# Attention rounds of five score units, the order of the expert tiles, and the end stage of a fused transformer block

## Chip, cores and metric

The kernel runs on one core of one Trainium2 chip. The metric is the device time of one execution in microseconds, lower is better. All times below are of that kind, or come from one profiled execution of the kernel.

## The reference

The inputs are `query` (1, 2048, 512) and the weights; everything is float32. Cut to what matters:

```python
xn = layernorm(x)
x = x + attention(xn, Wq, Wk, Wv, Wout, lambdas, rms_weight) + ffn(xn, gate, w1, w3, w2, sw1, sw3, sw2)

def attention(xn, ...):                       # H = 16 heads, two maps each, D = 16
    q, k = rotary(xn @ Wq), rotary(xn @ Wk)   # (T, 2H, D)
    v1, v2 = (xn @ Wv).reshape(T, H, 2, D)
    attn1 = softmax(causal(q1 k1 / sqrt(D))) @ [v1, v2]
    attn2 = softmax(causal(q2 k2 / sqrt(D))) @ [v1, v2]
    f = rfft(attn1, over T) - lambda_full * rfft(attn2, over T)
    a = irfft(f * gaussian(frequency))
    a = a * rsqrt(mean(a * a, per head) + eps) * rms_weight * (1 - lambda_init)
    return a.reshape(T, 512) @ Wout

def ffn(x, ...):                              # 8 experts, best 2 of each token, width 352
    y = sum of topk_w * w2[e] (silu(w1[e] x) * w3[e] x)
    return y + (silu(x @ sw1) * (x @ sw3)) @ sw2     # shared expert, width 704
```

## The kernel before, in words

There are three stages. The first (0 to about 210 us) does the layer norm, the gate, the routing of tokens to experts and the projections to q, k and v. The third, `ending`, does the filter over time as a folded transform, the norm per head, the output projection and the sums with the experts' results. The stage between, `middle`, mixes attention with the experts and is where most of the change lies. In it the order of the instructions on TensorE (PE), VectorE (DVE), ScalarE (ACT), GpSimd (POOL) and the queue of SyncE (SP) is as the program issues them; in `ending` the same holds for all but SP.

**Attention units.** The 32 chunks (8 groups of two heads by 4 blocks of 512 queries) give a stream of 544 *units*. A unit is mostly one head, one block of 128 keys and 512 queries, for both maps of the differential attention. `Chunk.scores` (L822) makes it with two matmuls of 64 rows, side by side in the array, into a tile `ps_s` of two PSUM banks (pool `sc_ps`, two tiles, so four banks). One exp on ACT (L835) writes `pt`, of which the pool `prob` has eight; units on the diagonal of the mask then have `affine_select` on POOL (L840). `Chunk.values` (L862) multiplies `pt` with v into `ps_o`, four matmuls of 32 columns for one key block. `Chunk.added` (L876, L879) sums the probabilities on DVE. At the end of a chunk, `sums` (L888, L893) and `finish` (L900 to L908: two transposes, a reciprocal, and `o_n`) normalize it, and `put` (L917, POOL) writes it over `vd`. After that `folded` (POOL) does, in small steps of a generator, the first butterflies of the transform for a finished group of heads.

**Experts.** The generator `experts` first does tiles of the shared expert (`wh` L246, tanh and products L256/L257/L263, `wy` L284) and then the 34 tiles of the routed experts: tiles 0 to 27 hold 128 tokens of one expert, tiles 28 to 33 hold 64 tokens each of two experts. A tile goes through `xT` (transposed rows, L165), `xh` and `xg` (L180), `ps_u` and `uT` (L206 to L209), `xy` (L216), `y_sb` (L225) and a store to `ys` (L228). There are two places for weights, `w_sb`; `fetch_up` (L146, `wu`, 1408 KB) and `fetch_down` (L149, `wd`, 768 KB) fill one from `wex` as soon as its last reader is done, on SP's queue, two fetches ahead. A tile of two experts uses both places. The generator yields a weight of work after each piece.

**Banks.** All the experts' results in PSUM (`xh`, `xg`, `ps_u`, `xy`, `ps_x`, and the attention's `ps_sum`, `ps_ot`, `ps_st`) rotate through three banks (pool `f_ps`, function `bank`). One bank is for `ps_o`.

**Rounds.** The loop at the end of `middle` takes the stream in rounds of four units: two units of scores (`burst(units[:2])`), the values of earlier units, the sums of a chunk that ends, two more units, the remaining values, then `put` and `finish`, then the adds on DVE, mixed with one or more steps of expert work, as many as keep the share of work done at the share of the stream done. The adds of unmasked units stand ahead of and between these steps, the masked ones behind them. Last come up to two steps of `folded`. Once attention has ended, the rest of the experts' steps follow without it.

**The end stage.** `ending` opens pools of its own over the memory of `middle`. It makes a last tile of the shared expert (`kept` holds its inputs), the products with the filter (`ps_z`, L1141) with butterflies on DVE around them, and then a loop of eight steps over pairs of output tiles: `prepared` (next pair: L1163, L1219, L1243 to L1254), `means` (L1223 to L1227), `scales` (L1234), `across` (transposes, L1262/L1264), `projected` (L1270) and `finished` (L1275, add and store). The residual and the experts' results arrive in tiles `res`, of which there are twelve: `fetched` loads the query rows on SP (L1120), adds `ysh` (L1123) and gathers twice from `ys` (L1125) with DMAs on POOL. `still` issues those of the last four tiles inside the loop.

Of the kernel before, what the change touches and what calls it, by code (L numbers as in the profile page):

```python
# [8 lines left out]
F32 = mybir.dt.float32  # L9
# [37 lines left out]

NP = (T * TOP // HALF - NX) // 2
WUP = NE * 2 * FI
WCOL = WUP + NF * E  # L50
# [17 lines left out]
def block_kernel(  # L68
# [527 lines left out]
    def middle(general):  # L596


        with ExitStack() as pools:
# [29 lines left out]
            def experts():  # L629
# [7 lines left out]
                for t0 in range(EARLY, NT - 1, TQ):  # L637
                    t1 = min(t0 + TQ, NT - 1)
                    last = t1 == NT - 1
                    cols = slice(t0 * P, t1 * P)  # L640
                    for n, us in enumerate(chunks(xnT[:, :, cols], u_last)):
                        if last and n == 0:
                            who_sb = mp.tile([P, E], F32, tag="x", name="who_sb")
                            who_sb = who_sb[:NR].rearrange("n (k p o) -> n k p o", k=TOP, o=2)
                            for k in range(TOP):
                                nc.sync.dma_start(who_sb[:, k], who[k][: NR * P, :].rearrange("(n p) o -> n p o", p=P))
                        elif last and n == 2:
                            nc.vector.tensor_add(who_sb[:, 0], who_sb[:, 0], who_sb[:, 1])
                        elif last and n == 3:
                            ps = bank([P, 2, NR], "ps_w")  # L650
                            for i in range(2):
                                nc.tensor.transpose(ps[:, i, :], who_sb[:, 0, :, i], ident[:NR, :NR])
                            nc.vector.tensor_copy(tok, ps[:, 0, :])
                            nc.vector.tensor_copy(wcol, ps[:, 1, :])
                        elif last and n == 5:


                            xr = [rows_of(0), rows_of(1)]
                            es = [routed(0)]
                            fetch_up(es[0], 0, nc.sync)  # L660
                        yield 3.45 * (t1 - t0) / TQ
                    if last:
                        es.append(routed(2))
# [20 lines left out]
                def tile_down(j, uT):  # L684
                    return places(j, 1), uT, ys[j * P : (j + 1) * P, :], wcol[:, j : j + 1]

                for j in range(NR):
# [5 lines left out]
                    if j + 2 < NR:  # L693
                        xr.append(rows_of(j + 2))
                    for n in sets[j]:
# [61 lines left out]
            def greatest(g, qc):  # L757
# [29 lines left out]
                return shift  # L787

            class Chunk:

# [19 lines left out]

                def scores(self, unit):

                    g, qc = self.g, self.qc
                    if general and not self.probs:
                        self.shift = greatest(g, qc)
                    ps = sps.tile([P, 2, QC], F32, tag="sc", name="ps_s")
                    for h, kb, off, col, w in unit:
                        for s in range(2):
                            r = slice(64 * s, 64 * s + 64)
                            k = keys[2 * g + h, kb // TQ][r, kb % TQ * P : (kb % TQ + 1) * P]  # L820
                            to = ps[:, s, col : col + w]
                            nc.tensor.matmul(  # L822
# [11 lines left out]
                    used = slice(min(c for *_, c, _ in unit), max(c + w for *_, c, w in unit))  # L834
                    nc.scalar.activation(pt[:, :, used], ps[:, :, used], AF.Exp, scale=SCALE)  # L835
                    for _, kb, _, col, _ in unit:
                        if kb >= qc * TQ and not general:

                            part = pt[:, :, col : col + P]
                            nc.gpsimd.affine_select(  # L840
                                out=part, in_=part, pattern=[[0, 2], [1, P]], compare_op=ALU.is_ge, fill=0.0,
                                base=0, channel_multiplier=-1,
                            )
# [147 lines left out]
            def burst(units):  # L991
                nonlocal begun
                found = []
                for n, chunk, unit in units:
# [21 lines left out]

            def masked(entry):
                _, c, unit = entry
                return any(kb >= c.qc * TQ for _, kb, *_ in unit)

            def added(entries):
# [6 lines left out]

            for i in range(0, len(stream), 4):
                units = stream[i : i + 4]  # L1030
                found = burst(units[:2])
# [19 lines left out]
                added(before)  # L1051
                added(u for u in units[:2] if not masked(u))
                later = [u for u in units[2:] if not masked(u)]
                while True:
                    work()
                    added(later[:1])
                    later = later[1:]
                    if worked / (work_all - left) >= (i + 4) / len(stream):
# [32 lines left out]
    def ending():  # L1091

        with tc.tile_pool(name="tail1", bufs=1) as t1, tc.tile_pool(name="tail", bufs=2) as tp, tc.tile_pool(
            name="tail_ps", bufs=4, space=PSUM
        ) as fps, tc.tile_pool(name="conv_ps", bufs=2, space=PSUM) as zps, tc.manual_schedule(
            engines={mybir.EngineType.PE, mybir.EngineType.DVE, mybir.EngineType.Activation, mybir.EngineType.Pool}
# [53 lines left out]
            def copied(z):  # L1152
                diff = tp.tile([P, 2, E], F32, tag="diff", name="diff")
                nc.scalar.copy(diff, z)
# [27 lines left out]
            product(zr[:, 1, :], [(1, vd[:, 1, :])])  # L1182
            first = tp.tile([P, E], F32, tag="first", name="first", bufs=1)
            nc.scalar.copy(first, zr[:, 1, :])
# [127 lines left out]
            for n in range(NT // 2):  # L1312
# [157 lines left out]
```

## Time and profile before

| what | value |
|---|---|
| time before, median of 3 | 1358.39 us (1357.41 to 1359.54) |
| profiled execution, its own time | 1360.14 us |
| its span | 1358.3 us |
| PE busy, share of the span | 1312.6 us, 97% |
| DVE, ACT, POOL busy | 74%, 51%, 46% |
| granted TensorE clock | 0.994 |
| HBM read and written | 169.69 MB and 43.10 MB |
| first stage, attention with experts, end stage | 0 to 210, 210 to 1241, 1241 to 1358 us |

The profile is of one execution. Busy time of an engine counts its instructions, not the issue of DMAs. PEld is the load of a matmul's weights, which runs beside PE. In the kernel's names, `ps_s<-qS,kS` means that `ps_s` is made from `qS` and `kS`; L822 is line 822 of the kernel before. A row that names a releaser tells whose end came last before the waiting instruction began.

### The profile page before, as it was taken

The numbers are of one execution on the slowest core, as the hardware profiler recorded it, in microseconds if no ns is written. First come the engines' busy times: TensorE is split into PE (matmuls) and PEld (weight loads), VectorE is DVE, ScalarE is ACT, GpSimd is POOL, SyncE is SP. The second block draws the span as 40 slices with busy tenths as digits, with TensorE's granted clock in tenths as the row PEclk, the third lists the DMA queues.
The fourth block names the chain that finished last, engine by engine and source line by source line (L and its number), as shares of the span: only waits on it lengthen the run. The fifth ranks groups of instructions, "written<-read, shape, count | busy, mean of one in ns | idle before, by whom it ended". The sixth has DMA issues, their size and how long they took to land.

```text
span 1358.3 us, 20810 instructions
## 1 busy us (share of the span) xinstructions
PE 1312.6 (97%) x7554; PEld 600.3 (44%) x7554; DVE 1005.4 (74%) x1344; ACT 688.4 (51%) x847; POOL 626.3 (46%) x671
## 2 busy tenths in 40 slices
PE   7999999999999999999999999899999999987998
PEld 3444444334443444445444444344544444443544
DVE  7049883287668778868889986778898788764785
ACT  2311110265656566676666666566676666640221
POOL 0002330012221323235968984778589469421764
PEclk9999999999999999999999999999999999998999
DMA  9406673200211122235665656555565666777997
GB/s 375 171 16 171 201 196 97 89 15 32 75 43 31 40 75 82 74 123 170 190 194 143 226 176 180 181 173 174 185 194 178 210 189 230 262 294 293 175 219 169
DMA packets 75578, 214.29 MB, mean 158 GB/s; under 512 B 12244, under 2 KB 12696, under 8 KB 69576
## 3 DMA queue, kind: packets, MB, share of 16 engines
q1 hardware_dynamic: 62744, 185.68, 41.7%
q0 software_dynamic: 11056, 22.78, 8.6%
q10 hardware_dynamic: 1664, 4.38, 0.9%
q8 instruction: 63, 1.03, 0.3%
q14 instruction: 51, 0.42, 0.1%
HBM read 169.69 MB, written 43.10 MB: 157 GB/s over the span
## 4 chain that ended last, share of the span: by engine, by line
PE 65%; DVE 6%; POOL 5%; DMA 3%; issue 1%; ACT 1%; SPq 0%; DVEq 0%; ACTq 0%; POOLq 0%
PE ps_o L862 16%; PE ps_s L822 12%; PE wh L246 8%; PE xy L216 6%; PE xg L180 5%; PE xh L180 5%; PE wy L284 4%; PE ps_sum L888 2%; DMA wu<-in_wex_dram 2%; POOL pt L840 1%; PE po L1270 1%; DMA wd<-in_wex_dram 1%; DVE sum L879 1%; PE ps_ot L900 1%; PE ps_x L165 1%
## 5 line engine op out<-in xcount | busy, mean ns | idle before, releaser
L879 DVE TENSOR_TENSOR sum<-sum,pt 128x1024 f32<-128x1024 f32 (+3 forms) x576 | 621.4, 1128 | 36.3 <-ACT pt L835 21.6
L835 ACT ACTIVATE pt<-ps_s 128x1024 f32<-128x1024 f32 x544 | 527.3, 1023 | 184.3 <-PE ps_s L822 131.0
L840 POOL TENSOR_SCALAR_AFFINE_SELECT pt<-pt 128x256 f32<-128x256 f32 x256 | 171.0, 693 | 358.7 <-ACT pt L835 357.5
L862 PE MATMUL ps_o<-pt,vd 128*32 128x512 f32 (+3 forms) x2560 | 268.0, 534 | 4.1 <-POOL pt L840 4.1
L822 PE MATMUL ps_s<-qS,kS 64*128 64x512 f32 (+3 forms) x1280 | 203.8, 406 | 2.0 <-DVEq L1335 1.6
L822 PEld LDWEIGHTS ps_s<-qS,kS 64*128 64x128 f32 x1280 | 97.1, 185 | 177.0 <-issue 95.9
L246 PE MATMUL wh<-xnT,wu 128*128 128x512 f32 (+1 forms) x352 | 150.4, 574 | 0.0
L862 PEld LDWEIGHTS ps_o<-pt,vd 128*32 128x32 f32 x2560 | 66.9, 109 | 125.8 <-issue 103.5
L545 PE MATMUL ps_x<-xnT,wqk_sb 128*128 128x512 f32 x256 | 110.5, 593 | 0.0
L498 POOL DMA_INDIRECT who<-pairs,slot x32 | 33.1, 1034 | 165.9 <-DVE pairs L495 104.9
L216 PE MATMUL xy<-wd,uT 128*128 128x512 f32 (+3 forms) x240 | 97.1, 606 | 7.7 <-DVE rcp L903 6.3
L246 PEld LDWEIGHTS wh<-xnT,wu 128*128 128x128 f32 x352 | 64.1, 190 | 72.7 <-issue 56.5
L180 PE MATMUL xh<-wu,xT 128*128 128x352 f32 (+1 forms) x320 | 90.5, 473 | 4.2 <-DMA wu<-in_wex_dram 3.3
L917 POOL TENSOR_TENSOR vd<-o_n 128x128 f32<-128x128 f32 x60 | 62.2, 1057 | 65.6 <-DVE o_n L908 65.5
L180 PE MATMUL xg<-wu,xT 128*128 128x352 f32 (+1 forms) x320 | 88.6, 468 | 0.0
L545 PEld LDWEIGHTS ps_x<-xnT,wqk_sb 128*128 128x128 f32 x256 | 48.4, 190 | 60.6 <-issue 60.6
L284 PE MATMUL wy<-wd,ws 128*128 128x512 f32 x160 | 74.8, 603 | 0.0
L257 DVE SCALAR_TENSOR_TENSOR ws<-ws,wh 128x512 f32<-128x512 f32 (+4 forms) x26 | 16.7, 644 | 73.6 <-ACT ws L256 73.6
L1125 POOL DMA_INDIRECT res<-ys,slot x32 | 54.9, 1715 | 25.3 <-DMA res<-ysh 13.5
L562 ACT CAST hi<-turned 128x1024 fp32r<-128x1024 f32 x16 | 16.7, 1045 | 93.9 <-DVE turned L560 70.9
L180 PEld LDWEIGHTS xh<-wu,xT 128*128 128x128 f32 (+1 forms) x320 | 48.0, 176 | 31.7 <-issue 6.5
L180 PEld LDWEIGHTS xg<-wu,xT 128*128 128x128 f32 (+1 forms) x320 | 46.6, 174 | 34.4 <-issue 14.8
(254 smaller groups left out, 1416.8 us busy)
## 6 DMA issues: line engine op xcount, KB each, us to landing
wu<-in_wex_dram SPq DMA_DIRECT2D x44, 1408.0 KB
wd<-in_wex_dram SPq DMA_DIRECT2D x43, 768.0 KB
kS<-parts_k SPq DMA_DIRECT2D x128, 128.0 KB
qS<-parts_q SPq DMA_DIRECT2D x256, 64.0 KB
ys<-y_sb SPq DMA_DIRECT2D x34, 256.0 KB
parts_q<-hi SPq DMA_DIRECT2D x32, 256.0 KB
parts_k<-hi SPq DMA_DIRECT2D x16, 256.0 KB
parts_k<-turned SPq DMA_DIRECT2D x16, 256.0 KB
```

The lines of the kernel that those rows point to most:

```text
L180: nc.tensor.matmul(dst[r, :], xT[:, c, r], w[:, o : o + FI], start=(c == 0), stop=(c == NE - 1), skip_group_check=True,)
L216: nc.tensor.matmul(y[r, :], uT[:m, ic, r], w[:m, ic * E : (ic + 1) * E], start=(ic == 0), stop=(ic == NF - 1), skip_group_check=True,)
L246: nc.tensor.matmul(dst, w_sb[o // WUP][0][:, o % WUP : o % WUP + P], x[:, c, :], start=(c == 0), stop=(c == NE - 1))
L284: nc.tensor.matmul(y, us[i][:, t * P : (t + 1) * P], w_sb[i // NF][1][:, i % NF * E : (i % NF + 1) * E], start=(i == 0), stop=(i == SCH - 1),)
L545: nc.tensor.matmul(ps[:, i, :], wqk_sb[st, qk][:, i, c, :], xnT[:, c, cols], start=(c == 0), stop=(c == NE - 1),)
L822: nc.tensor.matmul(to, k, queries[2 * g + h, qc][r, off : off + w], start=True, stop=not general)
L835: nc.scalar.activation(pt[:, :, used], ps[:, :, used], AF.Exp, scale=SCALE)
L840: nc.gpsimd.affine_select(out=part, in_=part, pattern=[[0, 2], [1, P]], compare_op=ALU.is_ge, fill=0.0, base=0, channel_multiplier=-1,)
L862: nc.tensor.matmul(self.o[r : r + 32, off:], vd[:, kb, v0 : v0 + 32], pt[:, s, :], start=first, stop=self.ended, skip_group_check=True,)
L879: nc.vector.tensor_add(to, to, pt)
L917: eng.tensor_add(vd[:, self.qc * TQ : (self.qc + 1) * TQ, v0 : v0 + 32], self.o_n[:, :, h, 0, :], self.o_n[:, :, h, 1, :],)
L1125: nc.gpsimd.indirect_dma_start(out=came[k], out_offset=None, in_=ys, in_offset=bass.IndirectOffsetOnAxis(ap=slot[:, step - 2, order[k] : o ...
```

## The change

**Rounds.** A round takes five units where no chunk is being closed (`closing` is empty), else four. The second burst then has three units, and the first of these is made "apart": its two score matmuls go to two banks of `f_ps` (`ps_a`) in place of a tile of `sc_ps`, and its exp is two instructions of one bank each. 84 rounds have five units; there are 115 rounds where there were 136.

**Adds and fold steps.** The adds of a round's first two units all stand ahead of the expert work, masked ones too. The steps of `folded` are one for an unmasked round and one more if the next four units are unmasked. A unit with two parts at columns 0 and 256 has one `affine_select` in place of two.

**Order of tiles.** `ORDER` puts the six tiles of two experts ahead of the last two tiles of one expert. One fetch of `wd` more is issued.

**End stage.** The tiles `ws`, `diff` and `first` come from a pool of their own, `tail2`, which is opened ahead of `tail`; `y_sb` is written by ACT; three operations of `prepared(4)` move to `prepared(3)`; in the loop, `finished` and `still` of an odd tile go ahead of `across` and `prepared`, and `means` goes behind `finished` of the even one. Nine of the sixteen `wh` products of the first group stand behind the last `xy` in PE's order; before, all sixteen stood ahead of it.

```diff
+ORDER = [*range(NP - 2), *range(NP, NR), *range(NP - 2, NP)]
...
-                sets = [[j] if j < NP else [2 * j - NP, 2 * j - NP + 1] for j in range(NR)]
-                halves = [2 * j + i for j in range(NR) for i in range(len(sets[j]))]
+                sets, halves = [], []
+                for tj in ORDER:
+                    n = 1 if tj < NP else 2
+                    sets.append(range(len(halves), len(halves) + n))
+                    halves += [2 * tj + i for i in range(n)]
...
-                    ps = sps.tile([P, 2, QC], F32, tag="sc", name="ps_s")
+                    if apart:
+                        banks = [bank([P, QC], "ps_a") for _ in range(2)]
+                    else:
+                        ps = sps.tile([P, 2, QC], F32, tag="sc", name="ps_s")
+                        banks = [ps[:, s] for s in range(2)]
...
-                    nc.scalar.activation(pt[:, :, used], ps[:, :, used], AF.Exp, scale=SCALE)
+                    if apart:
+                        for s in range(2):
+                            nc.scalar.activation(pt[:, s, used], banks[s][:, used], AF.Exp, scale=SCALE)
+                    else:
+                        nc.scalar.activation(pt[:, :, used], ps[:, :, used], AF.Exp, scale=SCALE)
...
-                    found += chunk.scores(unit)
+                    found += chunk.scores(unit, k == len(units) - 3)
...
-            for i in range(0, len(stream), 4):
-                units = stream[i : i + 4]
+            upto = 0
+            while upto < len(stream):
+                many = 4 if general or closing else 5
+                units = stream[upto : upto + many]
+                upto += many
...
-                added(u for u in units[:2] if not masked(u))
-                later = [u for u in units[2:] if not masked(u)]
+                added(units[:2])
+                later = [u for u in units[2:] if not masked(*u[1:])]
...
-                added(u for u in units if masked(u))
-                if any(map(masked, units)) or not shared:
-                    steps = 0
-                else:
-                    steps = 1 if any(map(masked, stream[i + 4 : i + 8])) else 2
-                for _ in range(steps):
+                added(u for u in units[2:] if masked(*u[1:]))
+                steps = [
+                    shared and not any(masked(*u[1:]) for u in some) for some in (units, stream[upto : upto + 4])
+                ]
+                for _ in range(sum(map(bool, steps))):
...
-            _, _, _, _, (_, _, stored), _ = expert(tp, fps)
-            hidden, gated, times, _, result = shared_expert(tp, fps, 2)
+            _, _, _, _, (_, _, stored), _ = expert(tp, fps, by_scalar=True)
+            hidden, gated, times, _, result = shared_expert(t2, fps, 2)
...
-                elif n == 4:
+                elif n == 3:
                     nc.vector.tensor_sub(dv, zw, dv)
                     scaled(v1[:, 0], dv[:, 1], TAN8, dv[:, 0])
                     scaled(v1[:, 1], dv[:, 0], -TAN8, dv[:, 1])
+                elif n == 4:
...
+                if ahead is not None:
+                    finished(2 * n - 1, ahead)
+                    still(2 * n - 1)
                 if n + 1 < NT // 2:
                     aT = across(2 * n + 2)
                 if n + 2 < NT // 2:
                     pairs.append(prepared(n + 2))
-                if ahead is not None:
-                    finished(2 * n - 1, ahead)
-                    still(2 * n - 1)
-                if n + 2 < NT // 2:
-                    pairs[n + 2].means()
                 if n + 1 < NT // 2:
                     now, po = po, projected(after)
                     finished(2 * n, now)
                     still(2 * n)
+                if n + 2 < NT // 2:
+                    pairs[n + 2].means()
```

More of the change, by code (lines that the diff above doesn't have):

```diff
@@ L655, in experts @@
                         elif last and n == 5:
-                            xr = [rows_of(0), rows_of(1)]
-                            es = [routed(0)]
+                            xr = [rows_of(j) for j in ORDER[:2]]
+                            es = [routed(2 * ORDER[0])]
                             fetch_up(es[0], 0, nc.sync)
@@ L662, in experts @@
                     if last:
-                        es.append(routed(2))
+                        es.append(routed(2 * ORDER[1]))
                         fetch_up(es[1], 1, nc.sync)
@@ L684, in tile_down @@
                 def tile_down(j, uT):
-                    return places(j, 1), uT, ys[j * P : (j + 1) * P, :], wcol[:, j : j + 1]
+                    tj = ORDER[j]
+                    return places(j, 1), uT, ys[tj * P : (tj + 1) * P, :], wcol[:, tj : tj + 1]
                 for j in range(NR):
@@ L693, in experts @@
                     if j + 2 < NR:
-                        xr.append(rows_of(j + 2))
+                        xr.append(rows_of(ORDER[j + 2]))
                     for n in sets[j]:
@@ L787, in greatest, with masked @@
                 return shift
+            def masked(chunk, unit):
+                return any(kb >= chunk.qc * TQ for _, kb, *_ in unit)
             class Chunk:
@@ L809, in units, with scores @@
                             yield [(h, kb, 0, 0, QC)]
-                def scores(self, unit):
+                def scores(self, unit, apart):
                     g, qc = self.g, self.qc
@@ L820, in scores @@
                             k = keys[2 * g + h, kb // TQ][r, kb % TQ * P : (kb % TQ + 1) * P]
-                            to = ps[:, s, col : col + w]
+                            to = banks[s][:, col : col + w]
                             nc.tensor.matmul(
@@ L834, in scores @@
                     used = slice(min(c for *_, c, _ in unit), max(c + w for *_, c, w in unit))
-                    nc.scalar.activation(pt[:, :, used], ps[:, :, used], AF.Exp, scale=SCALE)
-                    for _, kb, _, col, _ in unit:
-                        if kb >= qc * TQ and not general:
-                            part = pt[:, :, col : col + P]
+                    if apart:
[3 more added lines that the diff above has]
+                        nc.scalar.activation(pt[:, :, used], ps[:, :, used], AF.Exp, scale=SCALE)
+                    if masked(self, unit) and not general:
+                        cols = [col for *_, col, _ in unit]
+                        if cols == [0, 2 * P]:
+                            chosen = [pt.rearrange("p s (h q) -> p (s h) q", h=2)[:, :, :P]]
+                        else:
+                            chosen = [pt[:, :, col : col + P] for col in cols]
+                        for part in chosen:
                             nc.gpsimd.affine_select(
-                                out=part, in_=part, pattern=[[0, 2], [1, P]], compare_op=ALU.is_ge, fill=0.0,
-                                base=0, channel_multiplier=-1,
+                                out=part, in_=part, pattern=[[0, part.shape[1]], [1, P]], compare_op=ALU.is_ge,
+                                fill=0.0, base=0, channel_multiplier=-1,
                             )
@@ L993, in burst @@
                 found = []
-                for n, chunk, unit in units:
+                for k, (n, chunk, unit) in enumerate(units):
                     if n > begun:
@@ L1015, in work @@
                 worked += next(ex, work_all)
-            def masked(entry):
-                _, c, unit = entry
-                return any(kb >= c.qc * TQ for _, kb, *_ in unit)
             def added(entries):
@@ L1057, in middle @@
                     later = later[1:]
-                    if worked / (work_all - left) >= (i + 4) / len(stream):
+                    if worked / (work_all - left) >= upto / len(stream):
                         break
                 added(later)
-                added(u for u in units if masked(u))
-                if any(map(masked, units)) or not shared:
-                    steps = 0
-                else:
-                    steps = 1 if any(map(masked, stream[i + 4 : i + 8])) else 2
-                for _ in range(steps):
+                added(u for u in units[2:] if masked(*u[1:]))
[3 more added lines that the diff above has]
+                for _ in range(sum(map(bool, steps))):
                     if folding is None and ready:
@@ L1091, in ending @@
     def ending():
-        with tc.tile_pool(name="tail1", bufs=1) as t1, tc.tile_pool(name="tail", bufs=2) as tp, tc.tile_pool(
-            name="tail_ps", bufs=4, space=PSUM
-        ) as fps, tc.tile_pool(name="conv_ps", bufs=2, space=PSUM) as zps, tc.manual_schedule(
+        with tc.tile_pool(name="tail1", bufs=1) as t1, tc.tile_pool(name="tail2", bufs=2) as t2, tc.tile_pool(
+            name="tail", bufs=2
+        ) as tp, tc.tile_pool(name="tail_ps", bufs=4, space=PSUM) as fps, tc.tile_pool(
+            name="conv_ps", bufs=2, space=PSUM
+        ) as zps, tc.manual_schedule(
             engines={mybir.EngineType.PE, mybir.EngineType.DVE, mybir.EngineType.Activation, mybir.EngineType.Pool}
@@ L1152, in copied @@
             def copied(z):
-                diff = tp.tile([P, 2, E], F32, tag="diff", name="diff")
+                diff = t2.tile([P, 2, E], F32, tag="diff", name="diff")
                 nc.scalar.copy(diff, z)
@@ L1182, in ending @@
             product(zr[:, 1, :], [(1, vd[:, 1, :])])
-            first = tp.tile([P, E], F32, tag="first", name="first", bufs=1)
+            first = t2.tile([P, E], F32, tag="first", name="first", bufs=1)
             nc.scalar.copy(first, zr[:, 1, :])
```

## The prediction

> **What bounds the kernel now.** First the page: TensorE has 97% of the span, and the chain that ended last is mostly its own work.
>
> ```profile
> PE 1312.6 (97%) x7554; PEld 600.3 (44%) x7554; DVE 1005.4 (74%) x1344; ACT 688.4 (51%) x847; POOL 626.3 (46%) x671
> PE 65%; DVE 6%; POOL 5%; DMA 3%; issue 1%; ACT 1%; SPq 0%; DVEq 0%; ACTq 0%; POOLq 0%
> ```
>
> Second, the windows by stage (columns: window, length, then busy time and count for PE, PEld, DVE, ACT, POOL, then the granted clock, DMA share, GB/s). Up to 253 us both programs issue the same instructions.
>
> ```profile
> 600.00:1092.00 492.00, 481.56 (x3386) 231.78 (x3382) 413.49 (x487) 324.63 (x394) 365.49 (x389) 1.00 0.59 181
> 1092.00:1191.00 99.00, 98.11 (x739) 42.55 (x738) 81.21 (x96) 65.00 (x79) 66.75 (x67) 1.00 0.70 239
> 1191.00:1241.00 50.00, 42.39 (x310) 20.39 (x308) 30.45 (x70) 13.66 (x19) 7.71 (x10) 0.93 0.69 274
> 1241.00:1358.00 117.00, 103.02 (x328) 52.26 (x328) 78.48 (x125) 27.70 (x43) 69.63 (x48) 0.98 0.94 208
> ```
>
> The middle is bound by TensorE, with DVE at 84% (413.5/492) behind it; the stretch 1191 to 1241 has 7.6 us of idle PE and a reduced clock; the end has DMA at 94%. Third, the PE timeline: what a change of kind of matmul costs.
>
> ```profile
> 626.50 1.92 PE L862 MATMUL ps_o<-pt,vd 128*32 128x512 f32 x16
> 628.35 0.73 PE L822 MATMUL ps_s<-qS,kS 64*128 64x512 f32 x4
> ...
> 641.46 2.63 PE L180 MATMUL xg<-wu,xT 128*128 128x352 f32 x8
> 644.02 0.73 PE L822 MATMUL ps_s<-qS,kS 64*128 64x512 f32 x4
> ```
>
> In the unbroken part of such groups a 352-column matmul starts every 0.296 us and a group of four values every 0.429. Eight give 2.37, but scores start 2.56 after xg began: 0.19 too late. Four value groups give 1.72, but scores start 1.85 later: 0.13 too late. By start-to-start times over the whole middle: dense work to scores 0.093, scores to dense 0.096 net, scores to values 0.016, values to scores 0.113, values to dense 0.218. Two score units of a burst follow each other at 0.332 each, without such a cost.
>
> Fourth, the chain of waits around 1190 (start, duration, what).
>
> ```profile
> 1184.46 10.78 DMA wu<-in_wex_dram
> 1195.28 4.27 PE xh L180 x14
> ...
> 1206.44 10.38 DMA wu<-in_wex_dram
> 1216.87 2.60 PE xh L180 x14
> ...
> 1229.57 8.55 DMA wd<-in_wex_dram
> 1238.16 2.81 PE xy L216 x10
> 1241.04 0.70 ACT y_sb L225
> 1241.76 5.25 DMA ys<-y_sb
> 1247.12 0.39 ACT ws L256
> ```
>
> The last tiles, two experts each, wait for weights: once attention is over, nothing covers a 10 us fetch. Then the shared tile's tanh (ws) waits for the store of the last routed tile, and through it the fold and the convolution.
>
> **What the Trainium skill says.** "TensorEngine Tiling (Array Packing)", Tiling Modes, Key Properties: changing the tiling mode, not only the tile, drains TensorE. The trace agrees: scores are 64*128, values 128*32, expert work 128*128, and each change of kind costs the 0.09 to 0.22 us above. "TensorE: Matmul & The Clock Gate", Part 1: after an idle window of about 3.4 us the clock falls to half. It agrees: fourteen xh matmuls from 1195.28 take 4.27 us, 0.31 each, where the first of them are spaced 0.59 instead of 0.296. "Perfetto Trace Analysis", Optimizing Tensor Performance: independent groups should rotate through PSUM banks, so that one is emptied while the next is filled. This is what the added unit leans on: it takes two of three banks.
>
> **The change, part by part.**
>
> *Five-unit rounds.* 84 rounds have five units, so there are 115 rounds instead of 136, and score bursts fall from 272 to 230. Matmuls and columns are unchanged. Counted in the two instruction orders: dense to scores 152 to 124 (28×0.093=2.6), scores to dense 121 to 98 (23×0.096=2.2), scores to values 151 to 132 (0.3), values to scores 89 to 75 (14×0.113=1.6), values to dense 32 to 27 (5×0.218=1.1). Sum: **−7.8 us** of PE, wholly on the path.
>
> *The added unit's banks.* Its exp becomes two of 128x512 in place of one of 128x1024. ACT reads such a bank in 0.59 elsewhere (o_sb), so 2×0.59−1.02=+0.16, ×84=13.7 us, beside ACT's 66% in the middle: nothing, covered by PE; uncovered it would be 13.7. The unit's first matmul now waits for the readers of two banks: uT, xg, o_n and rcp on DVE 54 times, ACT 26 times (from the waits of the instruction order). Between the last write into such a bank and this reuse lie xh (2.4), two scores (0.66) and values (1 to 2.1), about 4 to 5 us. In the trace before, uT ends 1.6 us after its matmul (median), 3.8 at three quarters, 7.4 at most; o_n 1.6 and 4.8. So a few in a hundred are late, by 1 to 2 us. Queued behind a waiting score is the whole PE: the other two scores, values, xh. I take **+2**, from 0 to 10.
>
> *Adds and fold steps.* Masked adds of the first two units go ahead of the round's work. They wait on POOL's select; POOL's own queue holds fold steps in front of it. The sum of adds is unchanged, 576 for 621 us. A round with one step of expert work has 6.5 us of PE against 5×1.25+0.55=6.8 to 7.1 of DVE, but over 1.4 steps a round DVE stays at 88 to 89%. The merged selects (256 of 0.69 become 192 and 32 wider) are off the path, since POOL waits 357 us on ACT. The lone stalls of PE from 253 to 1190 sum to 18 us (late POOL pt, late uT). Taken as **0**, from −8 to +6: no row shows which of them move.
>
> *Tile order.* Two whole tiles now come last, so the six double tiles are fetched while attention runs. Of the 11.2 us stalled from 1191 to 1241, 8.9 wait on weights. In the new order each double tile's second fetch has 12, 13, 7, 14 and 12 us of PE work before its use; fetches took 10 to 10.4 undisturbed (11.8 behind the query loads in SP's queue, which stand ahead as before). The 7 us gap leaves a stall of 3 with 1.6 of half clock; the last whole tiles need single, early fetches. Hence 8.9−5=**−3.9**, from −9 to +3. One more wd fetch goes to a free slot behind everything: nothing; it shares rings with others for 8.5 us if not.
>
> *End stage.* (i) Nine of sixteen `wh` matmuls now follow the last xy: T, the end of the last xy, comes 1.0 earlier and the end grows by it. (ii) The separate pool takes away the ws wait: the fold on DVE then sets ps_z's start, a stall of about 2 instead of 4.4 (2.7 waiting and 1.7 of half clock; −2.4). y_sb moves from DVE (0.68) to ACT. (iii) 2.5 us of DVE work go from step 4 to step 3 and `finished` goes ahead of the next product: six loop stalls of PE, 5.9 together (2.0 of it the product waiting for `finished` at 1294.6), fall to about 2 (−3.8). The moved `still` issues its query load, ysh add and gathers earlier on SP and POOL. But these 6 us meet the gathers:
>
> ```profile
> POOL res L1123 <- DVE vd L1190: 40.1, 1, 40.1
> ```
>
> SP issues the query rows of `res` only once the last ys store has landed (1247.0, in both programs), and they take 5.4 us. POOL's first addition, idle for 40.1 before (the row names the DVE add that ended last before it), stands at 1252.6, T+11.8; the gathers then serve sixteen output tiles until 1350.7, T+109.9, and the last DVE add ends 1353.2. That chain is unchanged, at 94% DMA share, so only 0.7 to 1.9 us can be given back: **−2** after T, from −5 to +2; T's 1.0 counts whole as the gathers start with it: **−1**.
>
> Sum: −7.8+2+0−3.9−2−1=**−12.7**. The profiled execution is 1360.1 (span 1358.3), 1.7 above the median of 1358.4; so 1347.4 profiled and a median of **1345.7**.
>
> **Rivals.**
>
> *Banks bind (slower).* Every five-unit round waits for a late DVE reader. Without its own allowance the sum is −14.7, so from 0.18 us a round (84×0.18=15) there is no gain, and from 0.21 it is slower. At 0.25: 1358.4−14.7+21=1364.7. For it: three banks serve xh, xg, ps_u, xy, ps_x and now two more, and DVE is 84% busy. Against: the median reader is done in 1.6 us of 4 to 5. 13%.
>
> *Only the drains go.* The weights stay late (the 7 us gap grows, wd waits in their place) and the gathers hold the end: −7.8+2, so 1352.6. For it: DMA shares of 0.7 and 0.94. 20%.
>
> *More goes.* Fewer, longer rounds also take away half of the 18 us of lone stalls and the weights never stall: −12.7−5−5, so 1336 to 1340. For it: pt has a longer round to come in. 15%.
>
> *Masked adds block DVE.* In some 60 masked rounds DVE stands at an add until POOL's select, and uT behind it: at 0.15 us each +9, so 1355, within or near no change. 7%. That the change doesn't do what it says is excluded by the instruction orders.
>
> **The numbers.** My forecast 45%. A measurement tells about 0.2% (2.7 us) from no change. Faster by more: 45+20+15, and 1 of the last: 81%. Same: 6%. Slower: 13%. Range 1337 to 1359: most of the larger gain, and everything to no change; left out are the banks' rival and the largest gains.
>
> **What would show it.** Right: 115 pairs of bursts with the costs per change as before; PE busy in 600 to 1191 down by some 6; ps_a's waits on DVE under 5 us together; no wait on wu over 4 us after 1180; ws no longer waiting on ys; gathers ending 109 to 110 us after T. Wrong: ps_a at the head of PE's waits, on uT, xg or o_n; stalls of xh on wu growing before attention ends; or an end stage shorter than 115 us after T, which would say that the gathers never bound.

## The result, and the profile after

The changed kernel takes 1354.15 us (median of 18; the kernel before, measured beside it, 1359.55): ratio 0.9966, interval 0.9949 to 0.9982. That is 4.6 us faster, where 12.7 were forecast. The profiled execution took 1354.72 us, span 1353.0. Executions of one kernel differ by up to 14 us here, so verdicts below rest on the ratios, and profiles show where time lies.

The page of the kernel after, engines and chain:

```profile
PE 1302.2 (96%) x7554; PEld 607.5 (45%) x7554; DVE 1016.9 (75%) x1343; ACT 692.0 (51%) x932; POOL 614.2 (45%) x639
PE 59%; POOL 9%; DMA 8%; issue 2%; DVE 1%; ACT 1%; SPq 0%; POOLq 0%; DVEq 0%; ACTq 0%
```

PE has 10.4 us less work, but its share of the span fell: the span got only half of it. In the chain POOL and DMA rose: after the last xy it holds 46.8 us of DMA and 44.6 of POOL, the gathers most of all, where before it held 55.8 of DVE and 40.1 of PE. The windows by stage of the kernel after, with the columns of the prediction's table:

```profile
600.00:1092.00 492.00, 476.91 (x3313) 233.80 (x3314) 409.42 (x479) 321.74 (x430) 346.81 (x366) 0.99 0.59 182
1092.00:1191.00 99.00, 89.08 (x693) 37.69 (x693) 75.15 (x83) 57.53 (x78) 56.32 (x58) 0.93 0.70 249
1191.00:1237.00 46.00, 46.00 (x370) 24.74 (x369) 30.85 (x56) 20.79 (x30) 10.05 (x15) 1.00 0.80 286
1237.00:1353.00 116.00, 103.36 (x347) 53.35 (x346) 84.64 (x152) 28.48 (x44) 69.68 (x48) 1.00 0.97 215
```

The stretch after 1191 is now without idle PE, as meant; the idle time and the reduced clock (0.93) sit in 1092 to 1191. From 600 to 1092 PE idles 15.1 us of 492 where before it idled 10.4, at a clock of 0.99. A burst of three units in the PE timeline after:

```profile
699.63 2.74 PE L218 MATMUL xy<-wd,uT 128*128 128x512 f32 x6
702.30 0.50 PE L836 MATMUL ps_a<-qS,kS 64*128 64x512 f32 x2
702.64 0.62 PE L836 MATMUL ps_s<-qS,kS 64*128 64x512 f32 x4
703.19 1.06 PE L884 MATMUL ps_o<-pt,vd 128*32 128x512 f32 x8
```

It lasts 0.89 us (702.30 to 703.19), where two units took 0.66: the third adds only 0.23. Over all full-width bursts of three the median intervals are 0.337, 0.231 and 0.327, and over those of two 0.337 and 0.327. What PE waited for in the kernel after (from 252 us on; the longest rows):

```profile
PE xh L182 <- DMA wu<-in_wex_dram: 10.5, 4, 5.7
PE ps_s L836 <- DMA qS<-parts_q: 6.0, 5, 2.3
PE xh L182 <- DVE rcp L925: 2.6, 1, 2.6
PE xh L182 <- ACT xT L169: 2.5, 1, 2.5
PE ps_u L208 <- DVE xtanh L199: 1.8, 1, 1.8
```

The same of the kernel before, its three longest rows:

```profile
PE xy L216 <- DVE rcp L903: 6.3, 4, 3.3
PE ps_o L862 <- POOL pt L840: 4.1, 4, 1.6
PE xh L180 <- DMA wu<-in_wex_dram: 3.3, 2, 2.7
```

The row on qS is new: before, PE waited for no query load there. No row names `ps_a`, the tile in the experts' banks. The chain of the kernel after around 840, and SP's queue in the same stretch:

```profile
834.67 9.79 DMA wd<-in_wex_dram
844.48 1.93 DMA qS<-parts_q
```

```profile
834.67 0.33 SPq L151 DMA_DIRECT2D wd<-in_wex_dram  x1
835.10 9.68 SPq L745 DMA_DIRECT2D qS<-parts_q  x8
```

The wd fetch is issued at 834.67. The eight query loads behind it take SP 9.68 us to issue, the last of them at 844.48, when wd has landed; PE's scores start at 844.98 after 2.3 us of waiting. At 847.0 the clock falls to half for 3.4 us. By the semaphores in the trace each DMA of SP's queue waits, before it is issued, for the one that was issued eight DMAs earlier, and for the last query load that is the wd fetch. SP stood there before as well:

```profile
835.09 0.34 SPq L149 DMA_DIRECT2D wd<-in_wex_dram  x1
835.55 6.31 SPq L739 DMA_DIRECT2D qS<-parts_q  x8
```

There PE did not have to wait for these queries.

**A sum of PE's time from 252 us to the last xy.** I took each start-to-start time of matmuls, and split it at the median for the same pair of instructions: what exceeds it by over 60 ns is *lost* (waits, half clock), the rest is *work*. Before: 948.0 work, 41.0 lost. After: 932.3 work, 53.1 lost. So 15.7 us of work went and 12.1 came back as loss. The split depends on how the pairs are grouped: with one set of medians for all runs and the shapes kept apart, 14.4 went and 10.8 came back.

**The clock.** The mean granted clock over all runs is 0.994 before and 0.9886 after. An estimate of the time lost to it is (1 − clock) × time: 8 us before, 15.5 after. It is high, since it also counts half clock while PE is idle.

### The profile page after: what moved, and what is told of

Same layout as the page of the kernel before. It is cut to its first block, busy times and chain, and to the rows that moved or that the text cites. A ratio compares the mean times of both kernels' runs of the same rounds, so it can differ in the third digit from the quotient of the medians.

```text
span 1353.0 us, 20844 instructions
## 1 busy us (share of the span) xinstructions
PE 1302.2 (96%) x7554; PEld 607.5 (45%) x7554; DVE 1016.9 (75%) x1343; ACT 692.0 (51%) x932; POOL 614.2 (45%) x639
## 4 chain that ended last, share of the span: by engine, by line
PE 59%; POOL 9%; DMA 8%; issue 2%; DVE 1%; ACT 1%; SPq 0%; POOLq 0%; DVEq 0%; ACTq 0%
PE ps_o L884 16%; PE ps_s L836 9%; PE wh L248 8%; PE xh L182 6%; PE xg L182 5%; PE xy L218 5%; PE wy L286 4%; DMA wu<-in_wex_dram 3%; POOL res L1148 3%; PE ps_a L836 2%; PE ps_sum L910 2%; DMA res<-ys,slot 2%; POOL pt L862 1%; PE ps_ot L922 1%; DMA res<-ysh 1%
## 5 line engine op out<-in xcount | busy, mean ns | idle before, releaser
L901 DVE TENSOR_TENSOR sum<-sum,pt 128x1024 f32<-128x1024 f32 (+2 forms) x576 | 634.6, 1151 | 23.7 <-POOL pt L862 15.0
L853 ACT ACTIVATE pt<-ps_s 128x1024 f32<-128x1024 f32 x460 | 447.2, 1029 | 108.3 <-PE ps_s L836 69.3
L862 POOL TENSOR_SCALAR_AFFINE_SELECT pt<-pt 128x256 f32<-128x256 f32 (+1 forms) x224 | 183.8, 846 | 374.5 <-ACT pt L853 283.9
L884 PE MATMUL ps_o<-pt,vd 128*32 128x512 f32 (+3 forms) x2560 | 264.8, 535 | 1.8 <-POOL pt L862 1.7
L836 PE MATMUL ps_s<-qS,kS 64*128 64x512 f32 (+3 forms) x1082 | 166.5, 391 | 7.6 <-DMA qS<-parts_q 6.0
L836 PEld LDWEIGHTS ps_s<-qS,kS 64*128 64x128 f32 x1082 | 88.3, 186 | 94.8 <-issue 69.2
L851 ACT ACTIVATE pt<-ps_a 128x512 f32<-128x512 f32 x168 | 91.3, 596 | 54.2 <-PE ps_a L836 36.7
L182 PE MATMUL xh<-wu,xT 128*128 128x352 f32 (+1 forms) x320 | 97.0, 502 | 15.9 <-DMA wu<-in_wex_dram 10.5
L218 PE MATMUL xy<-wd,uT 128*128 128x512 f32 (+3 forms) x240 | 94.3, 598 | 0.1
L939 POOL TENSOR_TENSOR vd<-o_n 128x128 f32<-128x128 f32 x60 | 49.9, 850 | 62.4 <-DVE o_n L930 62.4
```

Source lines behind the costliest of these rows:

```text
L182: nc.tensor.matmul(dst[r, :], xT[:, c, r], w[:, o : o + FI], start=(c == 0), stop=(c == NE - 1), skip_group_check=True,)
L218: nc.tensor.matmul(y[r, :], uT[:m, ic, r], w[:m, ic * E : (ic + 1) * E], start=(ic == 0), stop=(ic == NF - 1), skip_group_check=True,)
L836: nc.tensor.matmul(to, k, queries[2 * g + h, qc][r, off : off + w], start=True, stop=not general)
L851: nc.scalar.activation(pt[:, s, used], banks[s][:, used], AF.Exp, scale=SCALE)
L862: nc.gpsimd.affine_select(out=part, in_=part, pattern=[[0, part.shape[1]], [1, P]], compare_op=ALU.is_ge, fill=0.0, base=0, channel_multip ...
L884: nc.tensor.matmul(self.o[r : r + 32, off:], vd[:, kb, v0 : v0 + 32], pt[:, s, :], start=first, stop=self.ended, skip_group_check=True,)
```

## The experiments

Ratios are to the kernel before. Where no other kernel is named, the edit is to the changed kernel. A difference between two of these kernels is good to about 3 us by their intervals.

**The parts, each taken back alone.**

```diff
-ORDER = [*range(NP - 2), *range(NP, NR), *range(NP - 2, NP)]
+ORDER = [*range(NR)]
```

> The changed kernel with the tiles in the order of before (double tiles last). Theory A, the new tile order costs: in the profile after, xh of the double tiles waits 0.6+5.7+2.2+2.0 us for wu between 1080 and 1151, with about 6 us of half clock behind it, where before paid 8.9 and 1.7 after 1190. With the old order back the early waits go and the late ones return: 4 to 7 us faster than the changed kernel, ratio to before about 0.991 to 0.994. Theory B, the order is worth what was forecast and the five-unit rounds are the loss: 3 to 5 us slower than the changed kernel, ratio 0.999 to 1.001.

Measured: 0.9989 (0.9976 to 1.0001), 3.1 us slower than the changed kernel. Theory A falls: over the runs the new order is worth 3.1 us, give or take 2.8, where 3.9 were forecast. (Its one profiled execution, span 1350.6, lies below its median of 1358.05; the runs go from 1351.9 to 1365.9.)

```diff
-                many = 4 if general or closing else 5
+                many = 4
...
-                    found += chunk.scores(unit, k == len(units) - 3)
+                    found += chunk.scores(unit, False)
```

> The changed kernel with four units in every round and no unit in the experts' banks; adds, tile order and end stage as changed. Theory A: the rounds save about 12 us of PE (42 bursts fewer, each with a change of kind before it, a slow second unit and a change behind it) and cost about 5 in waits, so this is 5 to 8 us slower than the changed kernel, ratio 1.000 to 1.003. Theory B, the waits of longer rounds (query loads, late DVE and ACT readers) eat all that the rounds save: the same as the changed kernel or faster, ratio 0.993 to 0.997, with no PE wait on qS between 700 and 1000.

Measured: 0.9987 (0.9976 to 0.9998), 2.9 us slower. Its sum is 946.6 work and 42.2 lost; so the rounds took away 14.3 us of work and brought 10.9 of loss (13.1 and 9.6 with the other grouping). Its mean clock is 0.9934, and PE waits for no query load. The time lies between the two theories: the work saved is about theory A's 12, the loss twice its 5.

The whole function `ending` of before:

> The changed kernel with the end stage of before. If the end stage brings what the two profiles show (1.75 us after the last xy, and about 1 before it by the wh products that moved): 2 to 3 us slower than the changed kernel, ratio 0.998 to 0.999, and ws waits for the ys store again for about 5 us. If the gathers alone set the end: the same as the changed kernel within 1 us, ratio 0.9966.

Measured: 1.0000 (0.9986 to 1.0014), 4.6 us slower. Its mean clock is 0.9863, so part of that may be the clock. The tile `ws` waits for the ys store again, for 6.2 us. From the last xy to the end its profile has 118.5 us, the changed kernel 115.6. In the profiles of all runs here this stretch is 114.9 to 117.6 us with the new end stage (median of fourteen 115.5) and 117.4 to 120.3 with the old one (median of six 119.0), so about 3.4 us are shown there.

**The rounds alone, on the kernel before** (the edits of the rounds, of `scores` and of `apart` from the diff above; adds and fold rule stay):

> The kernel before with the five-unit rounds alone (added unit in two of the experts' banks); order of adds, fold rule, tile order and end stage as before. Theory A: PE saves about 12 us, waits of 3 to 6 come in; ratio 0.993 to 0.995, faster than the changed kernel, since the order's cost is left out. Theory B: no gain, ratio 0.998 to 1.002, with waits of PE on qS, uT, rcp and xT of 10 us and more between 590 and 1190.

Measured: 1.0103 (1.0086 to 1.0119), 14 us *slower* than before, beyond theory B. So the rounds need something else of the change.

**The query loads.** A chunk of the first query block has five units. It was a round and a quarter, and is now one round; the queries of the next chunk are loaded when it begins.

```diff
             def load_queries(g, qc):
+                eng = nc.gpsimd if g > 0 and qc == NQC - 1 else nc.sync
...
-                            nc.sync.dma_start(
+                            eng.dma_start(
```

> The changed kernel with the query loads of each group's first chunk (7 chunks, 8 loads each) issued from POOL's queue in place of SP's. In the profile after, PE waits 6.0 us for qS at 721, 842 and 964, and half clock follows twice: a chunk of the first query block is one round of five units long, and the last of its eight loads stands on SP until the wd fetch issued before it has landed (844.48). Theory A, this is a part of what the longer rounds lose: the wait goes to under 1 us, 4 to 7 us faster than the changed kernel, ratio 0.992 to 0.994. Rival: the loads are late for the rings, not for the queue, or their issue delays POOL's selects: the same as the changed kernel or slower, ratio 0.996 to 1.000.

Measured: 0.9868 (0.985 to 0.9887), median 1342.17, 13 us faster than the changed kernel and the fastest of all. PE's waits in it, from 252 us on:

```profile
PE xh L182 <- DMA wu<-in_wex_dram: 7.7, 3, 3.4
PE ps_tr L1287 <- DVE a L1258: 5.3, 4, 2.1
PE ps_s L837 <- DMA qS<-parts_q: 3.5, 3, 1.6
```

The direct wait on qS fell by only 2.5 us, that on wu by 2.8. The larger part goes with the clock: half clock for 6.8 us in place of 27.3 in the two profiles (the last microseconds left out), and a mean of 0.995 in place of 0.9886 over the runs, up to 9 us by the estimate above. How much of that the queries cause is not shown: of the 27.3 us, 3.4 lie behind a wait for queries (at 847.0), 13.7 at waits for wu (1103 and 1151) and 6.8 at a wait for `xT` (602). The waits that remain are shorter (1.6 at most on qS).

The same edit on the kernel before:

> The kernel before with the query loads of each group's first chunk issued from POOL's queue. It has no PE wait on qS, and a mean granted clock of 0.994. Theory A, the late queries and the clock they cost belong to the five-unit rounds: no change within 0.2%, ratio 0.998 to 1.002. Rival: SP's queue delays the weights in both kernels, and moving the loads off it helps any kernel: ratio 0.988 to 0.992, as much as it helped the changed one.

Measured: 1.0004 (0.999 to 1.0017). Theory A: the loads cost nothing there. The same edit with the rounds, and with the tile order, taken back:

> The changed kernel with four units in every round and the query loads of each group's first chunk on POOL's queue. The run without the queries on POOL was at 0.9987. Theory A: still 0.997 to 0.999, so that with the queries in time the five-unit rounds (0.9868) are worth 14 to 16 us, about what the counted changes of kind and slow second units give. Rival: the queue helps here as well: 0.987 to 0.990, and the rounds are worth nothing much.

> The changed kernel with the tiles in the order of before and the query loads of each group's first chunk on POOL's queue. If the new tile order is worth the 3 to 4 us that were forecast: 0.989 to 0.991 against 0.9868. If its early waits for wu cost what the late ones did: 0.986 to 0.988.

Measured: 0.9951 (0.9932 to 0.997) with four units, 0.9938 (0.9913 to 0.9963) with the old order. In us, as differences of the ratios times 1359:

| worth of | queries on SP | queries on POOL |
|---|---|---|
| five-unit rounds | 2.9 | 11.3 |
| new tile order | 3.1 | 9.5 |

The first column is good to about 3 us by the intervals, the second to about 4. With the loads on SP's queue the rounds gain some 8 us less and the order some 6 less, each good to about 5. Read by rows, moving the loads is worth 13.3 us in the changed kernel, 4.9 with four units, 6.9 with the old order and nothing in the kernel before. With four units PE waits for no query load either way, so the longer rounds are not all of it: there the wait on wu fell from 8.4 to 6.4 us and half clock from 20.5 to 6.8.

Is it the number of loads? Four of 64 partitions in place of eight of 32:

```diff
-                        for rep in range(2):
...
+                        src = bass.AP(src.tensor, src.offset, [[D * T, 2], *[list(x) for x in src.ap]])
+                        nc.sync.dma_start(q[64 * s : 64 * s + 64, :].bitcast(F32), src)
```

> The changed kernel with the queries of a chunk in four loads of 64 partitions on SP's queue in place of eight of 32, the same bytes. If the loads were late since the last of eight stands on SP until an earlier fetch has landed: four are issued before that, the wait on qS falls to under 2 us, and the ratio is 0.986 to 0.992, as with POOL's queue. If SP's queue was not it (the rings are full of weights, and a load lands behind them whoever issues it): 0.995 to 0.998, with qS still waited for by 4 to 6 us.

Measured: 1.0764 (1.0746 to 1.0782), 108 us slower. The waits on qS are 48.9 us, and one load took 15.5 us to land. The edit also changed the form of the load (two blocks of 32 rows in one), so this run says nothing on the number of loads, and the number stays untested. And all chunks' loads on POOL:

```diff
-                eng = nc.gpsimd if g > 0 and qc == NQC - 1 else nc.sync
+                eng = nc.gpsimd if (g, qc) != (0, NQC - 1) else nc.sync
```

> The changed kernel with the query loads of all chunks but the very first on POOL's queue (31 chunks, 8 loads each). If SP's queue is what made them late, the weights gain a little more and the other chunks had slack: 0.984 to 0.988. If the 192 further loads on POOL delay its selects and fold steps: 0.988 to 0.996, with waits of PE on POOL's pt above 3 us.

Measured: 1.0113 (1.0089 to 1.0137), 33 us slower than with the first chunks' alone. Two rows of its waits point to why (with the first chunks' loads alone they are 51.5 and 15.2 us):

```profile
POOL qS L746 <- PE ps_s L837: 119.4, 20, 14.6
DVE sum L902 <- POOL pt L863: 30.1, 15, 7.9
```

The other chunks' loads wait for PE's last score on the buffer, and POOL stands with them; behind it stand the selects, DVE's adds and what PE wants from DVE.

**Adds, fold rule, selects.**

```diff
-                added(units[:2])
+                added(u for u in units[:2] if not masked(*u[1:]))
...
-                added(u for u in units[2:] if masked(*u[1:]))
+                added(u for u in units if masked(*u[1:]))
```

> The changed kernel with the masked adds of a round's first two units behind the expert work as before. Theory A, this order is the main part of what makes the five-unit rounds bearable: pt is freed a round's work earlier in the change; here exps wait for a free pt and DVE has up to five adds at a round's end, so 6 to 12 us slower than the changed kernel, ratio 1.001 to 1.005. Theory B: the same within 2 us, ratio 0.995 to 0.998.

Measured: 1.0002 (0.9986 to 1.0018), 4.9 us slower than the changed kernel. Its profile has PE waits on DVE of 3.1 (xy), 2.6 (ps_a for uT) and 1.9 us (ps_x) that the changed kernel lacks. The fold rule of before alone, and separate selects alone:

```diff
-                steps = [
-                    shared and not any(masked(*u[1:]) for u in some) for some in (units, stream[upto : upto + 4])
-                ]
-                for _ in range(sum(map(bool, steps))):
+                if any(masked(*u[1:]) for u in units) or not shared:
+                    steps = 0
+                else:
+                    steps = 1 if any(masked(*u[1:]) for u in stream[upto : upto + 4]) else 2
+                for _ in range(steps):
```

> The changed kernel with the fold rule of before alone (no fold step in a round with a masked unit). Theory A, the fold rule matters since fold steps pile up for the end: slower by 3 us or more, with fold steps (POOL or DVE vd) late before ps_z. Theory B, it is nothing: ratio within 0.001 of 0.9966. Should fold steps delay the selects of the next round, as the waits of PE on POOL's pt would show (1.7 us now), it is faster by 1 to 2 us.

```diff
-                        if cols == [0, 2 * P]:
-                            chosen = [pt.rearrange("p s (h q) -> p (s h) q", h=2)[:, :, :P]]
-                        else:
-                            chosen = [pt[:, :, col : col + P] for col in cols]
+                        chosen = [pt[:, :, col : col + P] for col in cols]
```

> The changed kernel with one select for each masked part (256 of two parts in place of 192 and 32 of four). The selects have 1.7 us of PE waits in the profile after. If they are off the path: ratio within 0.0015 of 0.9966. If the old adds' cost of 10 us was partly theirs (adds alone 5 us, fold rule minus 4): 3 to 9 us slower, ratio 0.999 to 1.003.

Measured: 0.9936 (0.9919 to 0.9953) and 0.9983 (0.9971 to 0.9995): 4.1 us *faster* with the old fold rule, 2.3 slower with separate selects, whose interval overlaps that of the changed kernel. With the queries on POOL the old fold rule gives nothing:

> The changed kernel with the fold rule of before and the query loads of each group's first chunk on POOL's queue. The old fold rule gave 0.9936, the queries 0.9868. If the two gains are apart: 0.983 to 0.985. If the fold steps only decided whether a query wait came at a bad moment for the clock: 0.986 to 0.988, the same as with the queries alone.

Measured: 0.9874 (0.9852 to 0.9895) against 0.9868. That fits its expectation's second case; no run shows how fold steps and query waits meet. All three as before, with the queries on SP and on POOL:

> The changed kernel with the adds' order, the fold rule and the one select for each part as before; rounds, tile order and end stage as changed. The rounds alone on the kernel before made it 14 us slower, and the changed kernel is 5 faster. Theory A, the adds and fold steps are what makes five-unit rounds bearable: 8 to 13 us slower than the changed kernel, ratio 1.002 to 1.006. Theory B, the rounds alone were slow for the old tile order and end stage: within 3 us of the changed kernel, ratio 0.995 to 0.999.

> The changed kernel with adds, fold rule and selects as before, and the query loads of each group's first chunk on POOL's queue. On SP's queue the old adds cost 10 us (1.0044 against 0.9966). If that cost was the late queries meeting late adds: 0.987 to 0.990, near the 0.9868 of the changed adds. If late adds hold the buffers by themselves: 0.993 to 0.997, and PE still waits for DVE (rcp, uT, xtanh) by 10 us.

Measured: 1.0044 (1.0027 to 1.006) and 0.9972 (0.996 to 0.9983): 10.6 us and 14.1 us slower than their partners. The old adds are thus a cause of their own, whichever queue the loads are on. One by one the three were 4.9, −4.1 and 2.3 us, so they do not add up. Of the second, PE waits beside those known:

```profile
PE xh L182 <- DVE sum L899: 4.0, 1, 4.0
PE xy L218 <- DVE rcp L923: 3.9, 2, 2.2
PE ps_o L882 <- POOL pt L860: 3.5, 4, 1.6
```

DVE stands at adds while PE wants results from it. The rounds alone on the kernel before, with the queries on POOL:

> The kernel before with the five-unit rounds alone, and the query loads of each group's first chunk on POOL's queue. On SP's queue the rounds alone were 14 us slower than before (1.0103). If the late queries are the cause: 0.992 to 0.997, faster than before, since PE's own work is 12 to 14 us shorter. If the adds behind the expert work are: 1.003 to 1.008.

Measured: 1.0043 (1.0027 to 1.006). Of the 14 us, the queries are 8. The other 6 are left with the queries in time; the old adds, which cost 14 us in the run before, are the likely holder, though this kernel also has the old tile order and end stage. Last, adds, fold rule and selects as changed on the kernel before, and nothing else:

> The kernel before with the order of adds, the fold rule and the one select for two parts as changed, and nothing else. Taken one at a time from the changed kernel, rounds, tile order and end stage are worth 2.9, 3.1 and 4.6 us, 10.6 together, but the whole change is worth 4.6. If the parts simply add, the adds with four-unit rounds cost what is missing: 4 to 7 us slower than before, ratio 1.003 to 1.005. If the adds are neutral there (the forecast's term of 0) and the parts get in each other's way: 0.999 to 1.001.

Measured: 1.0038 (1.0024 to 1.0052), 5.2 us slower. So these edits cost 5 us with four units (here) and are worth 11 with five (in the changed kernel, which also has the new tile order and end stage). Of where the 5 us are, nothing is shown: the profiled execution, span 1358.5, lies below its median by 4 us.

## Why the prediction was right or wrong

The direction held. The size did not: 4.6 of 12.7. The time lies in the range, near that of the rival "only the drains go" (1352.6), but that is luck: more work went than this rival has, and more waiting came. Two steps failed most: the price of a unit within a burst, and the waits that longer rounds bring, of which the prediction counted the banks alone. Taken back one at a time the parts are worth 2.9, 3.1, 4.6 and 10.6 us, 21 together, so they do not add up to the 4.6 of the whole.

*Five-unit rounds, −7.8: mechanism right, mis-sized.* The work saved is 14.3 us (13.1 by the other grouping). The step that failed is the sentence that two units of a burst follow each other at 0.332 "without such a cost". One unit follows another at 0.231; the first and the last interval of a burst, 0.337 and 0.327, each bear 0.10 of the change of kind. So a third unit costs 0.23 where the count of transitions priced it at 0.33. All score intervals together fell from 183.0 to 176.0 us in the two traces (work alone, by the other grouping). These 7 us and the 7.8 make 14.8, near what was measured.

*The added unit's banks, +2: no such wait.* In the profile after no PE wait names `ps_a`. The rival that ended slower, late readers at the banks, fell with it. With the old order of adds alone `ps_a` waits for uT by 2.6 us, with the old tile order by 0.8.

*Left out: the query loads.* This is the step that turned the gain: the rounds brought 10.9 us of loss (9.6 by the other grouping) where +2 was taken, and none of it at the banks. The prediction looked at SP's queue for what the weights wait for, not for what waits behind the weights, and wrote that the query loads "stand ahead as before". That a chunk of five units becomes one round, and leaves that much less time for the next chunk's queries, was to be read in `units()` and was not. Moving these loads gives 13 us, of which some 8 belong to the longer rounds.

*Left out: the clock.* Most of these 13 us is not the wait itself but goes with less half clock. Of the page "TensorE: Matmul & The Clock Gate" of the Trainium skill, Part 1, the prediction used the 3.4 us window only for stalls already there, and said that the trace agrees. It agrees on the half clock, but not on the length: that stall, before 1195.28, was 2.7 us long. In the profile after the clock fell at waits of 2.3 us (842) and 2.5 us (599), and after 2.65 us (746) it did not.

*Adds and fold steps, 0: wrong in size.* With five units they are needed: without them the changed kernel loses 10.6 us, more than the range (−8 to +6) allows. With four units they cost 5.2. The prediction named the wait of masked adds on POOL, and did not ask what adds behind the expert work do to DVE's other results.

*Tile order, −3.9: measured −3.1.* The sum was near and its terms were not. The prediction took 10 to 10.4 us for a fetch and one late weight, while the profile after has four waits on wu, 10.5 us. Two of them, 7.9 us, are for two fetches issued together, of which the second took 18 us:

```profile
1089.79 18.04 DMA wu<-in_wex_dram
1107.83 0.04 issue
1107.87 4.37 PE xh L182 x13
```

```profile
1073.34 8.01 SPq L745 DMA_DIRECT2D qS<-parts_q  x8
1081.39 2.37 SPq L733 DMA_DIRECT2D kS<-parts_k  x4
1083.87 1.24 SPq L230 DMA_DIRECT2D ys<-y_sb  x1
1085.36 2.24 SPq L151 DMA_DIRECT2D wd<-in_wex_dram  x1
1088.70 1.42 SPq L148 DMA_DIRECT2D wu<-in_wex_dram  x2
```

SP stood 8 us at query loads before it came to the wd fetch, and then wd and two wu ran side by side, at a DMA share of 1.00 from 1090 to 1100. So the step that failed is the undisturbed fetch: with double tiles fetched while attention runs, weights and query loads share the queue, and the weights run beside each other. The prediction's own sign of being wrong, stalls of xh on wu that grow before attention ends, came true. With these loads off the queue the order is worth 9.5 us, and the slower of the two fetches takes 12.6.

*End stage, −2 and −1: measured −4.6.* After the last xy about 3.4 us went, by the profiles of all runs, against the 2 forecast; the pair before and after shows 1.8. The gathers were not unchanged: in the profile after they end at T+106.2, not at 109 to 110 (102.7 to 111.9 over the profiles with the new end stage). That they cap the gain fits the chain, which after the last xy lies on DMA and POOL.

## What to carry to other kernels

When a round gets longer, list every load that is issued one unit of work ahead and ask how much time it now has, and what stands before it on the queue that issues it. Price a short stall of TensorE with the half clock that may follow, not by its own length. And try parts of a change together with the part they serve: the edits of adds, fold rule and selects cost 5 us alone and were worth 11 beside the longer rounds.

## What the runs showed of the hardware

- A stall of 2 to 3 us was followed by half clock for 3.4 us or a multiple of it in some cases and not in others, as shown above. Half clock was 6.8 to 34.1 us in the profiles of kernels with nearly the same work (the one with four loads apart). The time of the changed kernel varied by 14 us between runs (1349.4 to 1363.6), about 1.05 us for each 0.001 of mean clock; in the other kernels with fourteen runs or more it was 0.9 to 1.5.
- A load of 128 KB in the form 2×32 rows took 15.5 us to land in the chain of its kernel, where one of 64 KB and 32 rows took 7.0 in the chain of the kernel after, at 715.5.
- Between score units, one pair of matmuls starts 0.231 us after the other. The first interval of a burst is 0.337 and the last, to another kind, 0.327: a change of mode costs about 0.10 on each side within the burst.
